# Reordering the second half of a two-layer graph-attention round: layer 0's second products inside v's, v's last products woven with the features', norm and adjacency moved

## The chip, the core and the metric

The kernel runs on one NeuronCore of a Trainium2 chip. The metric is the device time of one execution in microseconds (us), the median over several runs. TensorE (PE) multiplies, VectorE (DVE), ScalarE (ACT) and GpSimd (POOL) do the rest of the arithmetic, and SyncE (SP) issues the transfers. Each engine has its own queue of instructions and meets the others through semaphores.

## The reference

There are 64 graphs of 256 nodes with 512 features. Each passes through two layers, and each layer is `x = layernorm(x + gnn(x))`:

```python
# layer 0: graph attention, 8 heads of 64
feats = einsum('bnf,hfu->bhnu', X, W)
dense = leaky_relu(e_self[..., :, None] + e_neigh[..., None, :], 0.2)
att   = softmax(dense + NEG_BIG * (1.0 - A), axis=-1)
out   = relu(einsum('bhij,bhju->bhiu', att, feats) + b)
# layer 1: attention with adjacency and distance terms
q, k, v = split(x @ W_qkv)
attn = softmax(q k^T * scale) * 0.33 + 0.33 * adj + 0.33 * exp(-dist)
out  = (attn @ v) @ W_out + b_out
x = layernorm(x + out)
```

Both the adjacency and the distance matrix of layer 1 are the input `adj`. Everything is float32.

## The kernel before

The kernel is a software pipeline over the 64 graphs, written out by hand. A round of the main loop (`for b in range(NB)`, L1035) calls `attention0_beside_projections1(b)` (L877) and then `attention1_beside_projections0(b)` (L950). In one round several graphs are under way: layer 0's attention of graph b (`attend0`), layer 1's projections of graph b-1 (`proj1`), layer 0's projections of graph b+1 (`proj0`), the softmax of layer 1 for graph b-1 (`softmax1`) and its weighted sum for graph b-2 (`attend1`).

The order of the source is the order of the machine. `do(stage, b, step, ...)` (L857) emits one step and then calls `in_order()` (L86), which ties each new instruction to the one before it on the same engine. So every `do` line is a place in up to five queues, and moving a line moves its instructions in all of them. A step whose graph number lies outside 0 to 63 does nothing, which is how the pipeline fills and empties.

The three projections (q and k, v, and layer 0's features) are each made of seven block products instead of eight, `p1` to `p7`, by `seven` (L281). Their results share three PSUM banks. The bank called "chain" takes p1, p6, p7, p4 one after the other on top of each other, and after each of the four ScalarE copies the running sum out:

```python
BANK = dict(p1="chain", p6="chain", p7="chain", p4="chain", p2="alone", p5="pair", p3="pair")
COPIES = dict(p1=11, p6=12, p7=22, p4=21)
ADDED = {11: "alone", 22: "pair", 12: "pair"}
```

So p6 cannot start before ScalarE has copied p1, and so on along the chain. The bank called "pair" takes p5; VectorE's `add 22` reads it, and p3 may only then be added to it; `add 12` reads the sum. `add 11` reads "alone", which is p2. An `add` also needs the copy into the block of the same number. Matmuls of all projections are at L292, the copies at L301, the adds at L304. In the profile the tiles are `pq_p` for q and k, `pv_p` for v and `pf_p` for the features.

The PSUM banks of these products form a ring of four (`ps_tile`); each round takes 16, the last one only to bring the ring round. Two larger buffers (`sc`) alternate between layer 0's products and layer 1's scores.

The other steps that matter here:

- `attend0`: `weights(h)` (L520) writes a head's unnormalised attention `pT` on VectorE. `product(g, t)` (L539) multiplies for half g of the heads and half t of the nodes on TensorE. `norm0(g, t)` (L552, L554) divides on VectorE. `end` (L563) applies the relu and the residual on VectorE and then starts the mean on GpSimd (L338). `squares` (L343) sums squares on ScalarE and then calls GpSimd for the reciprocal root and shift (L350, L353, L354). `norm` (L358) applies the layer norm on ScalarE.
- `proj1`'s `blocks` stores the normed rows to DRAM (`hs`) and loads them back in blocks (`hb`); `hT` transposes them on VectorE (L121) for the next round's q and k products.
- `proj0`: `xT` transposes the next graph's input on VectorE (L121) and forms four differences (L268 to L271). `aT` transposes its adjacency on VectorE. `far` makes two exponentials of it on ScalarE and casts the mask (L384, L385, L387). `shared` (L393 to L408) uses the result on VectorE.
- `attend1`: `weights(g)` multiplies the exponentials p of a pair of heads by the reciprocal sums `rb` and adds `ct`, on VectorE (L750, L757). `values(g)` (L767) multiplies them with v on TensorE, and ScalarE copies every second result (`oT`, L775). `project` (L828) is the output projection.
- `softmax1`: `scores(g)` (L668) on TensorE, followed by its exponentials on ScalarE (L677). `both(g)` (L689) adds halves on VectorE. There are two buffers for the scores, so scores 2 and 3 wait until the exponentials of scores 0 and 1 have read them.

`load`, `load_adj` and `load_rows` fetch the next graphs' inputs, one buffer each, on SyncE's queue, which issues in order: an issue that waits holds back those behind it.

Of the kernel before, what the change touches and what calls it, by code (L numbers as in the profile page):

```python
# [17 lines left out]
def kernel(  # L18
# [31 lines left out]
    NB, N, F = x.shape  # L50
# [35 lines left out]
    def in_order():  # L86

        new = []
        for ins in reversed(nc.cur_bb.bb.instructions):
            if ins.name in traced:  # L90
                break
            traced.add(ins.name)
            new.append(ins)
        for ins in reversed(new):
            if ins.engine in last:
                tc.add_manual_dep(
                    ins,
                    last[ins.engine],
                    mybir.DependencyInfo(
                        mybir.DependencyClass.NoSync, mybir.DependencyReason.DATA  # L100
                    ),
                    reason="order of the source",
                )
            last[ins.engine] = ins.name
# [6 lines left out]
    def load_blocks(dst, src):  # L111

        for q in range(Q):
            nc.sync.dma_start(
                dst[q * B : (q + 1) * B],
                src.rearrange("(k r) (c q s) -> q r c k s", r=B, q=Q, s=B)[q],
            )
# [7 lines left out]
    def load(b):  # L125

        XB[b] = io.tile([P, C, N // B, B], FT, tag="xb", name=f"xb_{b}", bufs=1)
        load_blocks(XB[b], x[b])

    def load_adj(b):  # L130
        ADJB[b] = io.tile([P, T, N // B, B], FT, tag="adj", name=f"adj_{b}", bufs=1)
        load_blocks(ADJB[b], adj[b])
        MROW[b] = io.tile([P, N], U8, tag="mask", name=f"mask_{b}", bufs=4)
        nc.sync.dma_start(MROW[b], nodemask[b].partition_broadcast(P))

    def load_rows(b):
        X[b] = io.tile([P, T, F], FT, tag="x", name=f"x_{b}", bufs=1)
        nc.sync.dma_start(X[b], x[b].rearrange("(t p) f -> p t f", p=P))
# [605 lines left out]
    def attend1(b):  # L744
# [108 lines left out]
        proj0=proj0, attend0=attend0, proj1=proj1, softmax1=softmax1, attend1=attend1  # L853
# [3 lines left out]
    def do(stage, b, step, *args):  # L857

        if 0 <= b < NB:
            if (stage, b) not in S:  # L860
                S[stage, b] = stages[stage](b)
            S[stage, b][step](*args)
            in_order()
# [13 lines left out]
    def attention0_beside_projections1(b):  # L877


        do("attend1", b - 3, "squares")  # L880
        do("proj1", b - 1, "qk", "p1")
        do("proj1", b - 1, "qk", "p2")
        if b > 0:
            do("proj0", b, "columns")
        do("proj1", b - 1, "qk", "p6")
        for h in range(HG):
            if b > 0:
                do("proj0", b, "scaled", h)
            do("attend0", b, "weights", h)
        do("attend1", b - 3, "store")  # L890
        do("proj1", b - 1, "qk_add", 11)
        do("proj1", b - 1, "qk", "p5")
        do("proj1", b - 1, "qk", "p7")
        do("attend1", b - 2, "residual")
        do("proj1", b - 1, "qk_add", 22)
        do("attend0", b, "product", 0, 0)
        if b > 0:
            for h in range(HG, H):
                do("proj0", b, "scaled", h)
        do("proj1", b - 1, "qk", "p4")  # L900
        do("attend0", b, "product", 0, 1)
        do("attend1", b - 2, "weights", 0)
        for h in range(HG, H):
            do("attend0", b, "weights", h)
        do("attend0", b, "norm0", 0, 0)
        do("attend0", b, "norm0", 0, 1)
        do("proj1", b - 1, "qk", "p3")
        do("proj1", b - 1, "qk_add", 12)
        do("attend1", b - 2, "weights", 1)
        do("proj0", b + 1, "xT")  # L910
        if b + 2 < NB:
            load(b + 2)
        do("proj1", b - 1, "values", "p1")
        do("proj1", b - 1, "values", "p2")
        do("proj1", b - 1, "v_add", 11)
        do("proj1", b - 1, "values", "p6")
        do("proj1", b - 1, "values", "p5")
        do("proj1", b - 1, "values", "p7")
        do("proj1", b - 1, "v_add", 22)
        do("proj0", b + 1, "aT")  # L920
        if b + 2 < NB:
            load_adj(b + 2)
        do("attend0", b, "product", 1, 0)
        do("proj1", b - 1, "values", "p4")
        do("proj0", b + 1, "far")
        do("attend0", b, "product", 1, 1)
        do("attend0", b, "norm0", 1, 0)
        do("attend0", b, "norm0", 1, 1)
        do("proj0", b + 1, "product", "p1")
        do("proj1", b - 1, "values", "p3")  # L930
        do("proj1", b - 1, "v_add", 12)
        do("attend0", b, "end")
        do("proj0", b + 1, "product", "p6")
        do("proj0", b + 1, "product", "p5")
        do("proj0", b + 1, "product", "p7")
        do("proj0", b + 1, "product", "p2")
        do("proj0", b + 1, "add", 11)
        do("attend0", b, "squares")
        do("proj0", b + 1, "add", 22)
        do("attend1", b - 2, "weights", 2)  # L940
        do("proj0", b + 1, "product", "p4")
        do("attend0", b, "norm")
        do("proj1", b, "blocks")
        if b + 1 < NB:
            load_rows(b + 1)
        do("proj0", b + 1, "product", "p3")
        do("proj0", b + 1, "add", 12)
        do("attend1", b - 2, "weights", 3)

    def attention1_beside_projections0(b):  # L950
# [84 lines left out]
    for b in range(NB):  # L1035
        attention0_beside_projections1(b)
        if b == 0:
            combine_weights1()
            in_order()
        attention1_beside_projections0(b)  # L1040
# [49 lines left out]
```

The softmax here doesn't subtract the row's maximum and nothing guards it: scores larger than these inputs give would overflow.

## Time and profile before

The three runs took 3255.54, 3258.58 and 3258.8 us; the median is 3258.58. The profiled execution spans 3256.7 us at a granted TensorE clock of 0.988.

| | share of the span or time |
|---|---|
| TensorE on the chain that ended last | 71% |
| ScalarE on that chain | 10% |
| GpSimd on that chain | 7% |
| VectorE on that chain | 6% |
| ScalarE busy | 1459.7 us (45%) |
| GpSimd busy | 317.8 us (10%) |
| one round, from 1602.27 to 1651.44 us | 49.17 us |
| TensorE busy in that round | 48.84 us |
| VectorE busy in that round | 41.17 us |
| ScalarE busy in that round | 22.77 us |

The shares of the chain come from the profile's list of what ended last, followed back from release to release. The rows on one round come from a table of busy time by stretch. A round is best read in the timeline, where an engine's instructions stand in order of time, merged as long as they are of one kind: start, length, engine, line, operation, output and inputs, shapes, count, and in brackets the idle time ahead of it and what ended that. In the round shown, TensorE does the q and k products from 1607.24 us on, v's from 1623.42, layer 0's second half-products at 1627.74 and 1630.39, the features' from 1632.12, and the values and scores of layer 1 from 1639.67 to 1647.9. TensorE's ends are modelled, and a matmul that waits for the one before or for its weights may still count as busy, so it is safer to compare starts.

### The profile page before, as it was taken

Reading aid. Unit: us, or ns where it says so; the run is one execution under the profiler, and the core shown is the slowest. Engines: PE = TensorE matmul, PEld = TensorE weight load, DVE = VectorE, ACT = ScalarE, POOL = GpSimd, SP = SyncE. Lnnn points to the kernel's source line nnn. Section 1 sums busy time; section 2 is a strip of 40 time slices with the busy share of each in tenths; the row PEclk is TensorE's granted clock in tenths of the full one; section 3 lists DMA queues with packets and bytes.
Section 4 is the critical chain, followed back from the end, with each engine's and each line's share of the span. In section 5 each row is a group of like instructions: output and inputs, shape, how many; then the busy total and the mean of one; then the engine's idle time right before and its main releaser. Section 6 shows DMA issues by size and latency. Waiting matters only on the chain.

```text
span 3256.7 us, 55552 instructions
## 1 busy us (share of the span) xinstructions
PE 3160.1 (97%) x21262; PEld 2497.4 (77%) x21262; DVE 2653.1 (81%) x5152; ACT 1459.7 (45%) x3585; POOL 317.8 (10%) x518
## 2 busy tenths in 40 slices
PE   4999999999999999999999999999999999999997
PEld 4877877877877877778778778778778778788774
DVE  6688888888888878888888888888888888888874
ACT  1344444454454444444444444444444444444442
POOL 0001101011011011011011010110110110110110
PEclk7999999999999999999999999999999999999998
DMA  7244343443343443443443443434434434434421
GB/s 155 69 115 99 99 115 92 105 115 90 105 115 86 109 113 86 108 106 94 113 105 92 115 96 102 115 92 106 115 87 109 110 89 110 113 86 108 108 76 53
DMA packets 764393, 331.86 MB, mean 102 GB/s; under 512 B 696672, under 2 KB 697440, under 8 KB 747744
## 3 DMA queue, kind: packets, MB, share of 16 engines
q1 hardware_dynamic: 764128, 328.30, 39.8%
q8 instruction: 169, 2.77, 0.3%
q14 instruction: 96, 0.79, 0.1%
HBM read 259.80 MB, written 68.16 MB: 101 GB/s over the span
## 4 chain that ended last, share of the span: by engine, by line
PE 71%; ACT 10%; POOL 7%; DVE 6%; DMA 4%; issue 2%; SPq 1%; ACTq 0%; DVEq 0%; POOLq 0%
PE pq_p L292 22%; PE av L539 12%; PE po L828 12%; PE pv_p L292 11%; PE pf_p L292 7%; PE pz L668 4%; ACT junk L343 3%; POOL rstd_l L353 3%; ACT x L358 3%; ACT p L677 2%; POOL rstd_l L350 2%; POOL shift_l L354 2%; PE pd L697 2%; DMA gb<-gs 1%; DVE pT L520 1%
## 5 line engine op out<-in xcount | busy, mean ns | idle before, releaser
L539 PEld LDWEIGHTS av<-v,pT 128*128 128x128 f32 x4096 | 493.9, 194 | 18.9 <-ACT v L485 12.5
L539 PE MATMUL av<-v,pT 128*128 128x65 f32 x4096 | 491.8, 274 | 12.2 <-ACT v L485 12.2
L292 PE MATMUL pq_p<-hC,wqk_sb 128*128 128x128 f32 x4096 | 482.9, 276 | 1.7 <-ACT qk L301 1.6
L292 PEld LDWEIGHTS pq_p<-hC,wqk_sb 128*128 128x128 f32 x4096 | 467.8, 192 | 3.4 <-ACT qk L301 3.2
L828 PE MATMUL po<-wo_sb,oT 128*128 128x512 f32 x1008 | 460.1, 600 | 0.0
L520 DVE SCALAR_TENSOR_TENSOR pT<-gb,ccol,at 128x256 f32<-128x256 f32 x1024 | 416.9, 479 | 25.0 <-ACT ccol L448 17.9
L292 PE MATMUL pq_p<-hT,wqk_sb 128*128 128x128 f32 x3072 | 379.1, 281 | 9.2 <-DVE hT L121 9.2
L292 PEld LDWEIGHTS pq_p<-hT,wqk_sb 128*128 128x128 f32 x3072 | 358.3, 194 | 35.7 <-DVE hC L270 22.2
L301 ACT COPY v<-pv_p 128x256 f32<-128x256 f32 x256 | 95.3, 372 | 560.8 <-PE pv_p L292 560.8
L828 PEld LDWEIGHTS po<-wo_sb,oT 128*128 128x128 f32 x1008 | 181.9, 190 | 204.6 <-issue 203.2
L757 DVE TENSOR_TENSOR p<-p,ct 128x1024 f32<-128x1024 f32 x256 | 313.6, 1225 | 8.7
L750 DVE TENSOR_TENSOR p<-p,rb 128x1024 f32<-128x1024 f32 x256 | 311.1, 1215 | 7.0 <-DMA rb<-rs 7.0
L677 ACT ACTIVATE p<-pz,hide 128x512 f32<-128x512 f32 x512 | 312.0, 707 | 2.0 <-PE pz L668 1.9
L343 ACT ACTIVATE junk<-x,nmean_l 128x512 bf16<-128x512 f32 x256 | 184.9, 722 | 271.8 <-POOL nmean_l L338 267.7
L668 PE MATMUL pz<-qk 64*128 64x256 f32 x2048 | 274.3, 397 | 21.5 <-ACT p L677 20.2
L358 ACT ACTIVATE x<-x,shift_l,rstd_l 128x512 f32<-128x512 f32 x256 | 193.9, 805 | 223.7 <-POOL shift_l L354 223.7
L338 POOL TENSOR_SCALAR nmean_l<-sums_l 128x2 f32<-128x2 f32 x128 | 28.7, 224 | 2612.0 <-DVE x L563 1639.1
L668 PEld LDWEIGHTS pz<-qk 64*128 64x128 f32 x2048 | 183.0, 187 | 114.6 <-ACT p L677 75.0
L292 PE MATMUL pf_p<-wf_sb,xC 128*128 128x264 f32 x1008 | 254.1, 396 | 7.8 <-ACT v L301 4.5
L485 ACT ACTIVATE v<-v 128x64 f32<-128x64 f32 x1024 | 258.6, 340 | 0.0
L767 PE MATMUL av<-p,v 128*64 128x256 f32 x2016 | 245.8, 386 | 2.7 <-DVE p L757 2.7
L292 PE MATMUL pv_p<-wv_sb,hC 128*128 128x256 f32 x1024 | 242.1, 379 | 0.0
(107 smaller groups left out, 3970.4 us busy)
## 6 DMA issues: line engine op xcount, KB each, us to landing
gb<-gs SPq DMA_DIRECT2D x64, 1028.0 KB
rb<-rs SPq DMA_DIRECT2D x64, 1024.0 KB, 4.6
x<-in_x_dram SPq DMA_DIRECT2D x64, 512.0 KB, 4.2
hs<-x SPq DMA_DIRECT2D x64, 512.0 KB
hb<-hs SPq DMA_DIRECT2D x256, 128.0 KB, 3.1
out_dram<-x SPq DMA_DIRECT2D x64, 512.0 KB, 3.0
xb<-in_x_dram SPq DMA_DIRECT2D x252, 128.0 KB, 3.7
adj<-in_adj_dram SPq DMA_DIRECT2D x256, 64.0 KB, 3.0
```

The costliest lines, as they stand in the source:

```text
L292: matmul(d, lhsT, rhs, start=(p in FIRST and i == 0), stop=(i == len(todo) - 1), skip_group_check=True,)
L343: nc.scalar.activation(junk, self.src[:, t, :], AF.Square, bias=self.nmean[:, t : t + 1], accum_out=self.rstd[:, t : t + 1],)
L358: nc.scalar.activation(self.src[:, t, :], self.src[:, t, :], AF.Identity, bias=self.shift[:, t : t + 1], scale=self.rstd[:, t : t + 1],)
L485: nc.scalar.activation(V0[b][:, t, h, :U], V0[b][:, t, h, :U], AF.Copy, scale=V0[b][:, t, h, U : U + 1],)
L520: nc.vector.scalar_tensor_tensor(pT[h][:, j, :], GB[b][:, h, :N], CCOL[b][:, j, h : h + 1], AT[b][:, j, :], op0=ALU.max, op1=ALU.mult,)
L539: matmul(av[:, k, :], pT[h][:, j, t * P : (t + 1) * P], V0[b][:, j, h, :UA], start=(j == 0), stop=(j == T - 1),)
L668: matmul(pz[:, r, j, :], QK[b][rows, g, 1, j * P : (j + 1) * P], QK[b][rows, g, 0, :], start=True, stop=True,)
L677: nc.scalar.activation(p[:, :, j, :], pz[:, :, j, :], AF.Exp, bias=hide[:, j, b : b + 1], scale=U**-0.5,)
L750: nc.vector.tensor_mul(p, p, REC[b][:, k : k + 2, g // 2, :] .unsqueeze(2) .to_broadcast([P, 2, T, N]),)
L757: nc.vector.tensor_add(p, p, CT[b].unsqueeze(1).to_broadcast([P, 2, T, N]))
L767: matmul(av[0][r * U : (r + 1) * U, g % 2, :], V1[b][:, j, 2 * g + r, :], PROBS[b][g][:, r, j, :], start=(j == 0), stop=(j == T - 1),)
L828: matmul(po, oT[:, c, t * P : (t + 1) * P], wo_sb[:, c, :], start=(c == 0), stop=(c == C - 1),)
```

## The change

Only the order of the steps in the second half of `attention0_beside_projections1` changes; no step is added, dropped or altered.

- Layer 0's two second half-products move from behind v's p7 and p4 to behind v's p2 and p5. Their `norm0` and `end` follow at once, ahead of v's `add 22`.
- v's last products are woven with the features' first ones: p7, features' p1, p4, features' p6, p3.
- Layer 0's `squares` come before the features' p7, and its `norm`, the store of its rows and the load of the next rows come before the features' p2.
- The features' `add 22` comes before `add 11`.
- The adjacency's transpose, the load of the next adjacency and `far` move from v's p7 and p4 to behind the features' `add 11`.
- The second layer's `weights 1` move from ahead of `xT` to behind v's `add 12`; `weights 2` from ahead of the features' p4 to behind their p3.

It is meant to start layer 0's norm earlier, so that what waits for it on ScalarE and in memory is free sooner, and to give each chain copy another product to hide behind.

```diff
-        do("attend1", b - 2, "weights", 1)
         do("proj0", b + 1, "xT")
         if b + 2 < NB:
             load(b + 2)
         do("proj1", b - 1, "values", "p1")
         do("proj1", b - 1, "values", "p2")
         do("proj1", b - 1, "v_add", 11)
+        do("attend0", b, "product", 1, 0)
         do("proj1", b - 1, "values", "p6")
         do("proj1", b - 1, "values", "p5")
-        do("proj1", b - 1, "values", "p7")
-        do("proj1", b - 1, "v_add", 22)
-        do("proj0", b + 1, "aT")
-        if b + 2 < NB:
-            load_adj(b + 2)
-        do("attend0", b, "product", 1, 0)
-        do("proj1", b - 1, "values", "p4")
-        do("proj0", b + 1, "far")
         do("attend0", b, "product", 1, 1)
         do("attend0", b, "norm0", 1, 0)
         do("attend0", b, "norm0", 1, 1)
+        do("attend0", b, "end")
+        do("proj1", b - 1, "values", "p7")
+        do("proj1", b - 1, "v_add", 22)
         do("proj0", b + 1, "product", "p1")
+        do("proj1", b - 1, "values", "p4")
+        do("proj0", b + 1, "product", "p6")
         do("proj1", b - 1, "values", "p3")
         do("proj1", b - 1, "v_add", 12)
-        do("attend0", b, "end")
-        do("proj0", b + 1, "product", "p6")
+        do("attend0", b, "squares")
+        do("attend1", b - 2, "weights", 1)
         do("proj0", b + 1, "product", "p5")
         do("proj0", b + 1, "product", "p7")
-        do("proj0", b + 1, "product", "p2")
-        do("proj0", b + 1, "add", 11)
-        do("attend0", b, "squares")
-        do("proj0", b + 1, "add", 22)
-        do("attend1", b - 2, "weights", 2)
-        do("proj0", b + 1, "product", "p4")
         do("attend0", b, "norm")
         do("proj1", b, "blocks")
         if b + 1 < NB:
             load_rows(b + 1)
+        do("proj0", b + 1, "add", 22)
+        do("proj0", b + 1, "product", "p2")
+        do("proj0", b + 1, "add", 11)
+        do("proj0", b + 1, "aT")
+        if b + 2 < NB:
+            load_adj(b + 2)
+        do("proj0", b + 1, "product", "p4")
+        do("proj0", b + 1, "far")
         do("proj0", b + 1, "product", "p3")
         do("proj0", b + 1, "add", 12)
+        do("attend1", b - 2, "weights", 2)
         do("attend1", b - 2, "weights", 3)
```

## The prediction

> **What bounds the kernel now.** I read the page first. TensorE is busy nearly all the time and VectorE four fifths of it:
>
> ```profile
> PE 3160.1 (97%) x21262; PEld 2497.4 (77%) x21262; DVE 2653.1 (81%) x5152; ACT 1459.7 (45%) x3585; POOL 317.8 (10%) x518
> ```
>
> Busy is not unstalled, so I looked for the round in the PE timeline: the `pr` transposes start at 1602.27 and 1651.44, a round of 49.17 us. From the `pr` of 171.24 to that of 3131.70 lie 60 rounds, 49.34 us each. Then the waits view, and PE's timeline from 1636 to 1648:
>
> ```profile
> PE pz L668 <- ACT p L677: 20.2, 63, 2.9
> PEld pf_p L292 <- DVE v L304: 29.4, 63, 0.8
> DVE hT L121 <- DMA hb<-hs: 8.1, 8, 2.6
> ```
>
> ```profile
> 1636.60 1.94 PE L292 MATMUL pf_p<-wf_sb,xT 128*128 128x264 f32 x8
> 1638.58 1.16 PE L292 MATMUL pf_p<-wf_sb,xC 128*128 128x264 f32 x4
> 1639.67 1.95 PE L767 MATMUL av<-p,v 128*64 128x256 f32 x16
> 1641.55 2.00 PE L668 MATMUL pz<-qk 64*128 64x256 f32 x16
> 1643.48 1.95 PE L767 MATMUL av<-p,v 128*64 128x256 f32 x16
> 1645.69 2.29 PE L668 MATMUL pz<-qk 64*128 64x256 f32 x16 [0.26 <-ACT p L677]
> 1647.91 0.70 PE L828 MATMUL po<-wo_sb,oT 128*128 128x512 f32 x1
> ```
>
> Compare starts of like blocks. A feature product (4 matmuls) costs 0.89 us: the twelve from 1633.93 to 1636.60 took 2.67. But p2, p4, p3 took 3.07 (1636.60 to 1639.67); about 0.09 of it is the change to 64-column weights, so 0.31 is lost. The first two value blocks took 1.88, the second two 2.21: 0.33 lost. The first scores took 1.93, the second 2.22: 0.29 lost. So a round loses 0.93 us at two places: before the features' p3 (its weight load waits for VectorE's `add 22`), and at scores 2 and 3, which wait for the exponentials of scores 0 and 1. The causes stand in the VectorE, ScalarE and GpSimd timelines:
>
> ```profile
> 1637.76 0.77 DVE L304 TENSOR_TENSOR v<-pf_p,v 128x264 f32<-128x264 f32 x2 [1.99 <-PE pf_p L292]
> 1638.45 1.22 DVE L750 TENSOR_TENSOR p<-p,rb 128x1024 f32<-128x1024 f32 x1
> 1639.70 1.23 DVE L757 TENSOR_TENSOR p<-p,ct 128x1024 f32<-128x1024 f32 x1
> 1640.84 0.42 DVE L304 TENSOR_TENSOR v<-pf_p,v 128x264 f32<-128x264 f32 x1
> 1641.18 1.21 DVE L750 TENSOR_TENSOR p<-p,rb 128x1024 f32<-128x1024 f32 x1
> 1642.43 1.22 DVE L757 TENSOR_TENSOR p<-p,ct 128x1024 f32<-128x1024 f32 x1
> ```
>
> ```profile
> 1642.48 1.52 ACT L358 ACTIVATE x<-x,shift_l,rstd_l 128x512 f32<-128x512 f32 x2 [3.49 <-POOL shift_l L354]
> ```
>
> VectorE idles 1.99 us for `add 11` (it waits for p2), with `add 22` behind it; ScalarE's in-order queue is blocked 3.49 us by the layer norm waiting on GpSimd, and the exponentials stand behind it.
>
> **What the Trainium skill says.** "TensorE: Matmul & The Clock Gate", section "Architectural detail: the array is 16× 32×32, not 1× 128×128": TensorE's queue pulls weight loads ahead of running matmuls, while ScalarE and VectorE are strict first-in, first-out. The trace agrees: a late `add 22` costs a matmul slot through the load, and one late norm holds back all of ScalarE. "Perfetto Trace Analysis", section "Identifying the Most-Contended Engine": matmul busy time is a poor measure; so here, since the 0.93 us mostly count as busy. "GPSIMD Engine Reference", section "2. Architecture": GpSimd's SBUF port is shared with VectorE. The power at L353 takes 1.69 us beside VectorE's L750/L757, 0.71 at 1610.31; but L750 and L757 keep 1.21 to 1.23 us. So GpSimd pays, not VectorE.
>
> **The change, part by part.** No instruction is added or removed, so each queue's work is the same; every wait moves. I walk one round from v's p1 at 1623.42, with the trace's durations: v product 0.864 us, feature product 0.89, an attention half-product with the slower matmul after it 1.785; a PSUM reader starts 0.20 us after the next matmul block starts.
>
> TensorE after: v p1, p2 to 1625.15; first half-product to 1626.88 (its 0.054 falls in p6); p6, p5 to 1628.66; second half-product to 1630.39; p7 1631.31; f p1 1632.20; v p4 1633.07; f p6 1633.96; v p3 1634.82; f p5, p7, p2, p4 to 1638.38; f p3 to 1639.27, plus 0.09 is 1639.36, if nothing waits.
>
> Does anything there wait? The pT of heads 4 to 7 are done at 1623.69, before 1625.15. Each ScalarE copy that a chain needs (p1 before p6, p6 before p7, p7 before p4) has one product in between, 0.86 to 0.89, for 0.20 + 0.37: the same spacing as now, without loss (0.02 to 0.1 to spare for the load). v's p3 needs v's `add 22` at about 1632.8: met.
>
> VectorE after: attend1's weights 1 (2.39 us) leave the stretch before xT, so xT starts at 1625.31; xT 1.27, differences 1.48, `v_add 11` 0.33 to 1628.39; norm0 (1,0) 0.56; norm0 (1,1) waits for the second half-product, 1630.59, to 1631.15; `end` 1.24 to 1632.39; `v_add 22` to 1632.73; idle to 1635.02 for v p3; `v_add 12` to 1635.36; weights 1 to 1637.75; f `add 22`, ended at 1638.18. The load of f p3 wants it at 1638.16 and can take it 0.1 later: the 0.31 loss is gone, narrowly. f `add 11` to 1638.44, aT 0.70 to 1639.14, `add 12` after f p3 (1639.47) to 1639.81, weights 2 to 1642.20, weights 3 ended at 1644.67.
>
> That is the new wait. Before, weights 3 ended at 1643.65 and values 3 wanted it at about 1644.4. After, the unstalled value blocks run 1639.36 to 1641.24, scores 0, 1 to 1643.17, values 2 to 1644.09; then values 3 waits from 1644.09 to about 1644.73, with 0.05 more for the unprefetched load: 0.69 us. Behind it stand scores 2, 3, the projection and the next round.
>
> ScalarE after: f p6's copy ends 1634.51, squares to 1636.2, f p7's copy at 1636.80 on time; GpSimd's three operations take 1.25 us alone and 3.66 beside L750 (both in the trace), so the norm ends between 1638.9 and 1641.4 (1644.0 now); f p4's copy, far (1.47 us, moved behind the norm) to 1643.2 at worst; copy of oT, exponentials of scores 0 and 1 done by 1644.95 and 1646.1. The stalled PE reaches scores 2 and 3 at 1645.74 and 1646.71: no wait. So the 0.33 and 0.29 go too.
>
> Sum per full round: 0.93 removed, 0.69 added: 0.24 saved; with `add 12` 0.08 later (the reader after p2 now starts later by that), 0.16. I take 0.20, times 61 rounds (b = 2 to 62): 12 us.
>
> Irregular losses: 49.34 - 49.18 (the undisturbed round) over 60 rounds is 9.8 us. In most of these rounds `rb<-rs` or `hb<-hs` lands late. At 1816.44 a late rb held VectorE 1.40 us, so aT, so far, and f p1's copy behind far:
>
> ```profile
> 1832.11 2.94 PE L292 MATMUL pf_p<-wf_sb,xC 128*128 128x264 f32 x12 [0.98 <-ACT v L301]
> ```
>
> After, far is behind every copy but p3's, VectorE has 2.3 us of idle before v p3 to absorb it, and hb is asked for 2.6 us earlier. I book 8 us of the 9.8.
>
> Ends of the program: rounds 0 and 1 wait on hT (5.40 and 3.85 us in the PE timeline), which comes 2.0 and 2.6 us sooner with the earlier norm. In the last round, without features, weights 1 to 3 come later (1.5 us), but scores 2 waited 2.94 us for the norm, which comes 2.4 us earlier; net some 3 us. Together 8.
>
> The load of adj moves behind the rows' load on SP: SP is free from 1650.2 to 1653.8 now, and its five issues take 3.3 us, so `gs` is not held. Nothing.
>
> 3258.6 - 12 - 8 - 8 = 3230.6; I say 3230.
>
> **The rivals.** (1) VectorE is late at f p3 by some 0.3 us more than walked (the margin there is 0.1): then p3 stalls as now, weights 3 slip by the same, and the 0.20 per round becomes -0.10: 3258.6 + 6 - 16 = 3249. (2) The other side: a delay of 0.7 us in the VectorE chain, from GpSimd's operations now lying on weights 1 or from semaphore waits, makes each round 0.5 us longer: +30 - 16, 3273, slower. Against it: L750 and L757 keep their time beside GpSimd. (3) Values 3 never waits, because VectorE's idle after v p3 is shorter than I say: all 0.93 come back, 57 + 16 = 73 us: 3186. Against it: v p3 is an ordered wait, and 9.3 us of VectorE work stand between it and values 3.
>
> **How the numbers follow.** My walk 0.72; rival 1 0.15; rival 2 0.07; rival 3 0.06. An error of 0.15 us per round, the size of the margins, is 9 us; with the one-off terms (16, give or take 6) the range is 3214 to 3250. Faster by over 0.2% (below 3252) is the walk, rival 3 and half to two thirds of rival 1: 0.87; same 0.06; slower 0.07.
>
> **What would show it.** After: no `[... <-ACT p L677]` at scores 2; a new PE wait at av L767 on DVE p L757 of some 0.6 us, 60 times; PEld L292 waiting for DVE v L304 near zero; f p1's copy never behind far; the norm at L358 waiting less, hs some 2.6 us earlier; undisturbed rounds of 48.94 to 49.02. A wait at f p3 would mean rival 1; a round above 49.3, rival 2.

## The result, and the profile after

The changed kernel takes 3227.07 us in the median (3225.8 to 3228.24), against 3258.69 for the kernel before in the same comparison. The ratio is 0.9904, with a 95% interval of 0.9887 to 0.9921: 31.6 us, or 1%, faster. The prediction was 3230 with a range of 3214 to 3250.

The list of what ended last shows what became of the layer norm. ScalarE and GpSimd held 10% and 7% of that chain before; now both round to 0%:

```profile
PE 86%; DVE 11%; DMA 1%; SPq 1%; issue 1%; ACT 0%; POOL 0%; ACTq 0%; DVEq 0%; POOLq 0%
```

Here is TensorE's timeline of the same stretch of a round. v's p1 starts at 1605.50 here, against 1623.42 in the round of before, so 17.92 has to be added to compare:

```profile
1618.68 1.94 PE L292 MATMUL pf_p<-wf_sb,xT 128*128 128x264 f32 x8
1620.46 1.05 PE L292 MATMUL pf_p<-wf_sb,xC 128*128 128x264 f32 x4
1621.44 1.95 PE L767 MATMUL av<-p,v 128*64 128x256 f32 x16
1623.32 2.00 PE L668 MATMUL pz<-qk 64*128 64x256 f32 x16
1625.24 1.08 PE L767 MATMUL av<-p,v 128*64 128x256 f32 x8
1626.82 1.08 PE L767 MATMUL av<-p,v 128*64 128x256 f32 x8 [0.49 <-DVE p L757]
1627.83 2.00 PE L668 MATMUL pz<-qk 64*128 64x256 f32 x16
1629.76 0.70 PE L828 MATMUL po<-wo_sb,oT 128*128 128x512 f32 x1
```

The features' p2, p4 and p3 now take 2.76 us from start to start (1618.68 to 1621.44), not 3.07. Scores 2 and 3 take 1.93 and carry no wait for exponentials. But the second pair of value blocks, 1.88 us of work, takes 2.59 (1625.24 to 1627.83): values 3 waits. Its reason stands in VectorE's timeline:

```profile
1619.83 0.76 DVE L304 TENSOR_TENSOR v<-pf_p,v 128x264 f32<-128x264 f32 x2
...
1621.55 0.43 DVE L304 TENSOR_TENSOR v<-pf_p,v 128x264 f32<-128x264 f32 x1 [0.34 <-PE pf_p L292]
1621.90 1.22 DVE L750 TENSOR_TENSOR p<-p,rb 128x1024 f32<-128x1024 f32 x1
...
1625.54 1.23 DVE L757 TENSOR_TENSOR p<-p,ct 128x1024 f32<-128x1024 f32 x1
```

Weights 3 end at 1626.77 and values 3 starts at 1626.82. Over the whole program, in the waits view of the changed kernel:

```profile
PEld av L767 <- DVE p L757: 61.4, 63, 2.4
PE av L767 <- DVE p L757: 32.8, 63, 1.9
```

So the new wait comes once a round. The undisturbed round (the median) is 48.95 us where it was 49.18. Measured by the starts of `pr` in the two profiled executions, the 31.3 us between them split as follows: 6.5 us up to the fourth `pr` (the pipeline fills), 13.7 us from 60 rounds shorter by 0.228 each, 9.2 us from irregular losses (what single rounds take beyond the undisturbed one) that fell from 9.8 to 0.6, and 2.0 us at the end.

### The profile page after: what moved, and what is told of

The parts are those of the page before. It is cut to its first block, busy times and chain, and to the rows that moved or that the text cites. A ratio compares the mean times of both kernels' runs of the same rounds, so it can differ in the third digit from the quotient of the medians.

```text
span 3225.4 us, 56184 instructions
## 1 busy us (share of the span) xinstructions
PE 3129.4 (97%) x21262; PEld 2496.2 (77%) x21262; DVE 2642.8 (82%) x5152; ACT 1480.9 (46%) x3585; POOL 248.5 (8%) x518
## 4 chain that ended last, share of the span: by engine, by line
PE 86%; DVE 11%; DMA 1%; SPq 1%; issue 1%; ACT 0%; POOL 0%; ACTq 0%; DVEq 0%; POOLq 0%
PE pq_p L292 25%; PE po L828 14%; PE av L539 14%; PE pv_p L292 12%; PE pf_p L292 12%; DVE p L757 5%; DVE p L750 5%; PE pz L668 4%; PE av L767 2%; PE pd L697 2%; PE pr L82 1%; DVE v L304 1%; SPq L236 0%; DMA gb<-gs 0%; PE po L810 0%
## 5 line engine op out<-in xcount | busy, mean ns | idle before, releaser
L520 DVE SCALAR_TENSOR_TENSOR pT<-gb,ccol,at 128x256 f32<-128x256 f32 x1024 | 416.8, 479 | 24.0 <-ACT ccol L448 17.9
L757 DVE TENSOR_TENSOR p<-p,ct 128x1024 f32<-128x1024 f32 x256 | 313.5, 1225 | 8.7
L750 DVE TENSOR_TENSOR p<-p,rb 128x1024 f32<-128x1024 f32 x256 | 311.5, 1217 | 7.7 <-DMA rb<-rs 7.6
L767 PE MATMUL av<-p,v 128*64 128x256 f32 x2016 | 260.0, 389 | 32.8 <-DVE p L757 32.8
L292 PE MATMUL pv_p<-wv_sb,hC 128*128 128x256 f32 x1024 | 259.3, 386 | 0.3 <-DVE v L304 0.3
L668 PE MATMUL pz<-qk 64*128 64x256 f32 x2048 | 256.9, 390 | 0.6 <-ACT p L677 0.6
L767 PEld LDWEIGHTS av<-p,v 128*64 128x64 f32 x2016 | 128.1, 136 | 149.4 <-DVE p L757 61.4
```

The source lines that it names most:

```text
L292: matmul(d, lhsT, rhs, start=(p in FIRST and i == 0), stop=(i == len(todo) - 1), skip_group_check=True,)
L520: nc.vector.scalar_tensor_tensor(pT[h][:, j, :], GB[b][:, h, :N], CCOL[b][:, j, h : h + 1], AT[b][:, j, :], op0=ALU.max, op1=ALU.mult,)
L668: matmul(pz[:, r, j, :], QK[b][rows, g, 1, j * P : (j + 1) * P], QK[b][rows, g, 0, :], start=True, stop=True,)
L750: nc.vector.tensor_mul(p, p, REC[b][:, k : k + 2, g // 2, :] .unsqueeze(2) .to_broadcast([P, 2, T, N]),)
L757: nc.vector.tensor_add(p, p, CT[b].unsqueeze(1).to_broadcast([P, 2, T, N]))
L767: matmul(av[0][r * U : (r + 1) * U, g % 2, :], V1[b][:, j, 2 * g + r, :], PROBS[b][g][:, r, j, :], start=(j == 0), stop=(j == T - 1),)
```

## The experiments

Theory at this point, as in the prediction: three losses of the kernel before are gone (0.31 us at the features' p3, 0.33 and 0.29 at scores 2 and 3), and one of about 0.7 has come in their place, VectorE's chain into values 3. The rivals: the losses of before are not as I divided them; the moves of the weights are what pays; far's place is what counts. "Round" below is the median distance of two `pr` transposes in the profiled execution. The kernel before took 3256.5 to 3258.9 us beside each of these runs, so times of different runs can be set side by side.

### Weights 1 back in front, weights 2 into VectorE's idle time

The changed order with these edits:

```diff
+        do("attend1", b - 2, "weights", 1)
         do("proj0", b + 1, "xT")
...
-        do("attend0", b, "end")
         do("proj1", b - 1, "values", "p7")
         do("proj1", b - 1, "v_add", 22)
+        do("attend0", b, "end")
...
-        do("attend1", b - 2, "weights", 1)
+        do("attend1", b - 2, "weights", 2)
...
         do("proj0", b + 1, "add", 12)
-        do("attend1", b - 2, "weights", 2)
         do("attend1", b - 2, "weights", 3)
```

> The changed order, but with layer 1's weights 1 back ahead of xT, weights 2 where weights 1 had been put (behind v's add 12), and v's add 22 ahead of the layer 0 end. Theory (in the changed kernel the only steady loss on TensorE, 0.71 us a round, is values 3 waiting for weights 3 on VectorE): weights 3 end some 2.4 us sooner, values 3 does not wait, a round takes 48.24 us instead of 48.95, and the time is about 3184 us. Rival A (the exponentials of scores 0 and 1 are the next wait, right behind): scores 2 and 3 wait again and most of the 0.71 us stays, about 3215 to 3227. Rival B (the norm, 0.5 us later on VectorE, sets the end): no better than 3227.

Measured: 3186.68 us, ratio to before 0.9779 (0.9766 to 0.9793), a round of 48.24. Its TensorE timeline has no wait left in this stretch, and the second pair of value blocks takes 1.88 us again:

```profile
1603.49 2.00 PE L668 MATMUL pz<-qk 64*128 64x256 f32 x16
1605.41 1.95 PE L767 MATMUL av<-p,v 128*64 128x256 f32 x16
1607.29 2.00 PE L668 MATMUL pz<-qk 64*128 64x256 f32 x16
```

The whole 0.71 us a round came back, as expected if the wait for weights 3 was the one steady loss of this stretch. This version beats both kernels: 2.2% below before, 40 us below the changed one. Its irregular losses are 1.1 us, although weights 1 stand in front again.

### The change without its moves of the weights

```diff
+        do("attend1", b - 2, "weights", 1)
         do("proj0", b + 1, "xT")
...
-        do("attend1", b - 2, "weights", 1)
...
             load_adj(b + 2)
+        do("attend1", b - 2, "weights", 2)
...
         do("proj0", b + 1, "add", 12)
-        do("attend1", b - 2, "weights", 2)
         do("attend1", b - 2, "weights", 3)
```

> The changed order without its moves of layer 1's weights: weights 1 ahead of xT and weights 2 behind the features' add 11 and aT, as in the kernel before. Theory: weights 2 and 3 still run mostly after v p3, but only 4.9 us of them; weights 3 end about 1626.1 on the changed kernel's clock, where values 3 wants them at 1625.95 to 1626.16; a wait of about 0.2 us is left, and v's p3 may wait 0.1 us for add 22; a round of 48.5 us, about 3200 us. Rival (the moves of the weights are what pays for the gain): slower than 3227.

Measured: 3191.66 us, ratio 0.9793 (0.978 to 0.9807), round 48.24. The direction is as expected; the waits of 0.2 and 0.1 us that I had left in do not show. The 60 rounds hold 7.2 us of irregular losses, though, where the changed kernel has 0.6. In each of its ten disturbed rounds TensorE stands at v's p3, which waits for `add 22`. So the moves of the weights cost 35 us net within the change, and what they gave for it is that late transfers hardly matter any more. The first experiment has nearly the same without them: there `add 22` stands ahead of layer 0's `end`, and 1.1 us are lost.

### Only the moves of the weights, in the kernel before

```diff
-        do("attend1", b - 2, "weights", 1)
         do("proj0", b + 1, "xT")
...
         do("attend0", b, "end")
+        do("attend1", b - 2, "weights", 1)
...
-        do("attend1", b - 2, "weights", 2)
...
         do("proj0", b + 1, "add", 12)
+        do("attend1", b - 2, "weights", 2)
         do("attend1", b - 2, "weights", 3)
```

> The kernel before with only the moves of layer 1's weights: weights 1 behind the layer 0 end, weights 2 behind the features' add 12. Theory: p3 waits 0.3 us longer for add 22, and values 3 waits for weights 3 some 0.6 us, while scores 2 and 3 wait no more; a round gains about 0.37 us, 23 us in all, less some 6 us of irregular waits that the slack on VectorE ahead of aT takes away: 3270 to 3282. Rival (VectorE's weights are hidden, only the norm counts): 3258 or faster.

Measured: 3274.19 us, ratio 1.0047 (1.0034 to 1.0059), round 49.58. The round is 0.40 longer (0.37 expected), and the irregular losses fall from 9.8 to 0.1 us although far stays where it was. Which transfer is late stands in VectorE's rows, at L443. First a long round of the kernel before (50.15 us), then an undisturbed one (49.58) of this run:

```profile
1069.78 0.18 DVE L443 TENSOR_TENSOR nd<-v,gb 128x16 f32<-128x16 f32 x1 [2.87 <-DMA gb<-gs]
```

```profile
531.19 0.19 DVE L443 TENSOR_TENSOR nd<-v,gb 128x16 f32<-128x16 f32 x1 [2.67 <-DMA gb<-gs]
```

Usually this wait is 1.2 us. Of the 16 rounds of before that are over 0.08 us too long, eight have `gb<-gs` late by 0.5 to 2.1 us (5.8 us lost in them), five `hb<-hs` (2.1 us) and one `rb<-rs` (1.2 us); the other two lose 0.6 us. Here `gb` is late by 0.6 to 1.8 us in eight rounds, which lose 0.2 us together. So weights 1 behind the end of layer 0 is enough to make the kernel nearly indifferent to a late transfer.

### Only the order of two adds, in the kernel before

```diff
         do("proj0", b + 1, "product", "p7")
+        do("proj0", b + 1, "add", 22)
         do("proj0", b + 1, "product", "p2")
         do("proj0", b + 1, "add", 11)
         do("attend0", b, "squares")
-        do("proj0", b + 1, "add", 22)
```

> The kernel before with one edit: the features' add 22 ahead of add 11 (and ahead of p2). Theory: the 0.31 us that the features' p3 loses goes, but TensorE then waits that much longer at scores 2 and 3 for the exponentials, which stand behind the layer norm on ScalarE; the time stays at 3258 us within 3. Rival (the losses add up, each is worth its own 0.31 us a round): 3240 us.

Measured: 3233.28 us, ratio 0.9918 (0.9904 to 0.9931), round 48.77. Both expectations fell. I had said nothing would come of it; one moved line brings 25.6 us, more even than the 19 of the rival. The norm must have ended earlier, and it did: it starts 18.65 us after v's p1 (1627.26 less 1608.61), against 19.06 before (1642.48 less 1623.42). These 0.41 us are the gain of the round: on TensorE the 0.31 us ahead of p3 are gone, and the second values and scores, which still wait for the exponentials, lose 0.52 us instead of 0.62. GpSimd's timelines say why the norm moved. First the kernel before, then this one:

```profile
1638.82 0.90 POOL L350 TENSOR_SCALAR rstd_l<-rstd_l 128x2 f32<-128x2 f32 x1 [2.74 <-ACT junk L343]
1639.80 1.69 POOL L353 TENSOR_TENSOR rstd_l<-rstd_l,mhalf 128x2 f32<-128x2 f32 x1
1641.57 0.88 POOL L354 TENSOR_TENSOR shift_l<-nmean_l,rstd_l 128x2 f32<-128x2 f32 x1
```

```profile
1624.01 0.48 POOL L350 TENSOR_SCALAR rstd_l<-rstd_l 128x2 f32<-128x2 f32 x1 [2.74 <-ACT junk L343]
1624.58 1.69 POOL L353 TENSOR_TENSOR rstd_l<-rstd_l,mhalf 128x2 f32<-128x2 f32 x1
1626.35 0.88 POOL L354 TENSOR_TENSOR shift_l<-nmean_l,rstd_l 128x2 f32<-128x2 f32 x1
```

and VectorE's rows of this one beside them:

```profile
1623.23 1.21 DVE L750 TENSOR_TENSOR p<-p,rb 128x1024 f32<-128x1024 f32 x1
1624.48 1.22 DVE L757 TENSOR_TENSOR p<-p,ct 128x1024 f32<-128x1024 f32 x1
...
1625.96 1.22 DVE L750 TENSOR_TENSOR p<-p,rb 128x1024 f32<-128x1024 f32 x1
```

Compare ends. L350 ends at 1624.49, VectorE's L750 at 1624.44. L354 ends at 1627.23, the next L750 at 1627.17. In the kernel before L350 ends at 1639.72 and L750 at 1639.67. I looked at all of them: of the instructions at L350 and L354 that overlap one of VectorE's L750 or L757, 125 of 125 in the kernel before end 50 ns (to the nearest 10) after it. L353 ends some 0.57 us after the one it overlaps at its start. So GpSimd's three small operations do not take a fixed time beside VectorE, as I had priced them; each is held until the L750 or L757 of the moment has ended, and the norm goes when the third of them has. As long as the three fall on the same instructions, whatever shifts weights 2 shifts the norm, the exponentials and scores 2 and 3. `add 22` behind the wait of `add 11` had delayed weights 2 by 0.41 us.

### A useless instruction ahead of weights 2, in the kernel before

The new theory makes an odd forecast. If VectorE is kept on something that does not hold GpSimd while L350 runs, one weights instruction fewer lies before the norm.

```diff
         do("proj0", b + 1, "add", 22)
+        probe(b)
         do("attend1", b - 2, "weights", 2)
```

Here `probe` issues `nc.vector.tensor_reduce(t, bo_bc[:, :384], AX.X, ALU.max)` in rounds 2 to 62; nothing reads `t`.

> The kernel before plus one useless VectorE instruction a round (a maximum over 128x384 into one column, about 0.57 us) just ahead of layer 1's weights 2. New theory after swap_only (the norm ends late because GpSimd's L350, L353 and L354 each have to wait until VectorE's running L750 or L757 ends; in every profiled run so far L350 and L354 ended 50 ns after it): L350 now finishes in the gap ahead of L750, one L750/L757 fewer lies before the norm, which ends some 0.9 us sooner although VectorE has more to do; scores 2 and 3 wait no more, a round takes 48.56 to 48.66 us and the time is 3222 to 3232 us: an added instruction makes the kernel faster. Rival A (GpSimd follows weights 2, whatever lies ahead): every round 0.57 us longer, 3293. Rival B (VectorE's delay is hidden, and the norm takes its fixed time): 3259.

Measured: 3216.91 us, ratio 0.9872 (0.9859 to 0.9886), round 48.55. The added instruction makes the kernel 40 us faster. VectorE and then GpSimd in this kernel:

```profile
1617.91 0.54 DVE L881 TENSOR_REDUCE probe<-bo_bc 128x1 f32<-128x384 f32 x1
1618.37 1.22 DVE L750 TENSOR_TENSOR p<-p,rb 128x1024 f32<-128x1024 f32 x1
1619.62 1.23 DVE L757 TENSOR_TENSOR p<-p,ct 128x1024 f32<-128x1024 f32 x1
```

```profile
1618.28 0.19 POOL L350 TENSOR_SCALAR rstd_l<-rstd_l 128x2 f32<-128x2 f32 x1 [2.74 <-ACT junk L343]
1618.55 1.60 POOL L353 TENSOR_TENSOR rstd_l<-rstd_l,mhalf 128x2 f32<-128x2 f32 x1
1620.23 0.67 POOL L354 TENSOR_TENSOR shift_l<-nmean_l,rstd_l 128x2 f32<-128x2 f32 x1
```

L350 takes its 0.19 us in the shadow of the reduction, L353 is held by the first L750, and L354 ends 50 ns after L757 (1620.90 and 1620.85), not after the next L750. The norm starts 18.05 us after v's p1, 1.0 us earlier. The features' p2, p4 and p3 still take 3.07 us here (1616.06 to 1619.13) and the second values and scores 1.88 and 1.92: the 0.63 us of the round are the scores' loss alone. That the hold exists is shown. What in L750 and L757 makes it is not: they read two SBUF inputs and the reduction one, and the Trainium skill's "GPSIMD Engine Reference", section "1. Specifications", names VectorE instructions with two SBUF inputs, or in a mode with two ports, as those that contend. The traces agree with that, though no run was made to vary it alone. In the changed kernel L354 runs inside the transpose of the adjacency, which has one input, in all of 61 overlaps, and keeps its 0.20 us; the 0.22 us of L338 fall into v's `add 22`, which has one of its two inputs in PSUM, 63 times, and are not stretched either:

```profile
1620.51 0.70 DVE L121 STREAM_TRANSPOSE adjT<-adj 128x512 f32<-128x512 f32 x1
```

```profile
1620.56 0.20 POOL L354 TENSOR_TENSOR shift_l<-nmean_l,rstd_l 128x2 f32<-128x2 f32 x1
```

In the kernel with the two adds swapped, L354 fell three times inside yet another instruction with two SBUF inputs (L253, L393 and L520, of 1024, 512 and 256 columns) and each time ended 54 to 55 ns after it. At L393:

```profile
114.38 0.68 DVE L393 TENSOR_TENSOR ct<-adjT,far 128x512 f32<-128x512 f32 x1
```

```profile
114.45 0.67 POOL L354 TENSOR_TENSOR shift_l<-nmean_l,rstd_l 128x2 f32<-128x2 f32 x1
```

So neither the length of L750 and L757 nor anything peculiar to them is needed.

### The same two adds, put back in the changed kernel

```diff
-        do("proj0", b + 1, "add", 22)
         do("proj0", b + 1, "product", "p2")
         do("proj0", b + 1, "add", 11)
+        do("proj0", b + 1, "add", 22)
```

> The changed kernel with the features' add 22 back behind add 11. Theory: here the norm no longer sets the end but VectorE's chain into values 3 does; p3 waits 0.31 us for add 22, add 12 and weights 2 and 3 slip by the same: a round of 49.26 us, 3246 us. Rival (the wait at values 3 swallows the wait at p3): 3227.

Measured: 3247.13 us, ratio to before 0.9972 (0.996 to 0.9984), round 49.27. That is 0.32 us a round over the changed kernel: here the swap is worth its own stall at p3, because the norm no longer lies on the path. The same edit is worth 0.41 us where the norm sets the end and 0.32 through the weight load where it does not.

### A useless addition on VectorE, late and early in the changed kernel

Here `probe` issues `nc.vector.tensor_add(t, bo_bc, bo_bc)`, 128x512, in rounds 2 to 62. First late, behind the features' p3:

```diff
         do("proj0", b + 1, "add", 12)
+        probe(b)
         do("attend1", b - 2, "weights", 2)
```

> The changed kernel plus one useless 128x512 VectorE addition a round (0.61 us by the rows of that size) between the features' add 12 and weights 2. Theory (VectorE's chain from p3 through weights 3 sets values 3): each of 61 rounds longer by 0.61 us, 3264 us. Rival (VectorE has slack there): 3227.

Measured: 3263.73 us, ratio to before 1.002 (1.0012 to 1.0029), round 49.55: 0.60 longer. Then early, where VectorE waits for v's p3:

```diff
         do("proj1", b - 1, "v_add", 22)
+        probe(b)
         do("proj0", b + 1, "product", "p1")
```

> The changed kernel plus the same useless addition between v's add 22 and add 12, where VectorE sits idle 1.68 us for v's p3. Theory: nothing, 3227 us within 3. Rival (VectorE's total work sets the time): 3264.

Measured: 3228.87 us, ratio to before 0.9914 (0.9901 to 0.9928), round 48.95, unchanged. The same instruction, 0.68 us long in its record with its overlap, costs 0.60 us a round behind p3 and nothing ahead of v's p3.

### The weave undone, in the changed kernel

```diff
         do("proj1", b - 1, "v_add", 22)
-        do("proj0", b + 1, "product", "p1")
         do("proj1", b - 1, "values", "p4")
-        do("proj0", b + 1, "product", "p6")
+        do("proj0", b + 1, "product", "p1")
         do("proj1", b - 1, "values", "p3")
         do("proj1", b - 1, "v_add", 12)
+        do("proj0", b + 1, "product", "p6")
```

> The changed kernel without the weave of v's last products: p7 and p4 stand together again with no other product between, then the features' p1, v's p3, the features' p6. Theory (each link of a chain costs a ScalarE copy: 0.20 us to its start and 0.37 us, hidden only by one product in between): p4 waits about 0.62 us and loses 0.1 more on its unprefetched weights, all behind it slips by the same, VectorE's chain into values 3 too: 0.73 us a round, 3271 us. Rival (the slip is taken up by the wait at values 3): 3227.

Measured: 3274.31 us, ratio to before 1.0055 (1.004 to 1.007), round 49.68: 0.73 over the changed kernel, as worked out. That is what one uncovered link of a chain, p7 to p4, costs here.

### far back beside v's products, in the changed kernel

```diff
         do("proj1", b - 1, "v_add", 22)
+        do("proj0", b + 1, "aT")
+        if b + 2 < NB:
+            load_adj(b + 2)
         do("proj0", b + 1, "product", "p1")
         do("proj1", b - 1, "values", "p4")
+        do("proj0", b + 1, "far")
...
-        do("proj0", b + 1, "aT")
-        if b + 2 < NB:
-            load_adj(b + 2)
         do("proj0", b + 1, "product", "p4")
-        do("proj0", b + 1, "far")
```

> The changed kernel with aT and far back where they were beside v's products (aT behind v's add 22, far behind v's p4). Theory: aT is free there, but far's 1.47 us now stand on ScalarE between the copies of v's p4 and the features' p6; the features' p7 waits about 0.4 us, squares and the copies behind them slip, p4 waits some 0.3 us more, and with it p3, add 12 and values 3: a round of 49.4 to 49.6 us, 3252 to 3268 us. Rival (far's place does not matter): 3227.

Measured: 3249.32 us, ratio to before 0.9975 (0.9965 to 0.9984), round 49.25: 0.30 over the changed kernel, where I had 0.45 to 0.65. ScalarE copies the features' p6 1.3 us later, behind far, and p7 waits for that; the second wait, at p4, is nearly hidden. The irregular losses stay at 0.6 us, so with weights 1 in their later place they do not depend on far's.

## Why the prediction was right

**The walk of the round held to a few hundredths where it counts.** On the clock of the prediction (17.92 added), f `add 22` ended at 1638.17 (1638.18 predicted), weights 3 at 1644.69 (1644.67), and values 3 started at 1644.74 (1644.73). The norm ended at 1640.23, between the two bounds given. The round shrank by 0.228, between 0.16 and 0.24; I took 0.20. That makes 13.7 us over 60 rounds (12 over 61 predicted). One step of VectorE's walk was wrong. `norm0 (1,0)` was to run at 1628.39, ahead of the second half-product; it waited for it, as it does in the kernel before, and began at 1630.59. So v's `add 22` ended at 1633.34, not 1632.73, and the idle time ahead of v's p3 was 1.68 us, not 2.3. That idle time took up the error; that it was there to do so was foreseen, the error was not.

**The price of the new wait was right and is shown.** The late and early probes, and weights 1 and 2 taken out of the chain into values 3, all came within 3 us of what that chain predicts.

**The losses removed were right in sum and wrong as separate causes.** I treated the 0.31 at p3 and the 0.62 at scores as independent and GpSimd's 3.66 us as a fixed price "beside L750". In the kernel before they are tied: the late `add 22` also delays weights 2, and weights 2 and 3 hold GpSimd and with it the norm. The swap alone showed it, the added reduction confirmed it. The forecast did not depend on it, because the change takes the norm off the path altogether: its bound of 1641.4 for a slow GpSimd still left the exponentials on time.

**The irregular losses were sized well, and their causes were half misnamed.** I booked 8 us, 9.2 came. I said that `rb<-rs` or `hb<-hs` lands late in most of these rounds and showed one with `rb`; in the kernel before that is the only one, and `gb<-gs` is the late transfer in half of them. Where it holds VectorE up, though, the path is the one I gave, by the adjacency and far to the copy of the features' p1, and the size came near. Of the two remedies that I named, far's place does not matter once weights 1 stand later. With the weights moved alone the losses go, so the slack that weights 1 leave on VectorE is enough. It is not the only way: with weights 1 in front and `add 22` ahead of layer 0's `end`, 1.1 us are lost. For `hb` the run with the added reduction speaks: there the norm comes 1.0 us earlier, weights 1 keep their place, and none of the 60 rounds waits for `hb` by more than 0.3 us, against five in the kernel before.

**The ends**: 8 us booked, 8.5 measured (6.5 at the start, 2.0 at the end); the split was 5 and 3.

None of the rivals came about. The margin that rival 1 turned on was narrow but sufficient: the weights of p3 loaded without a wait, and putting `add 22` back produced the stall that it feared.

## What to carry to other kernels

When an engine's order is fixed by hand, walk the two or three chains around the moved lines with the durations of the trace, and look first at what the change leaves last: here it took 0.93 us off a round and put 0.71 back, because weights 2 and 3 were moved behind a product that ends late. With weights 1 left in front, weights 2 put into VectorE's idle time and `end` behind `add 22`, the new order gave 72 us where the change gave 32. A stall seen at one instruction may also be feeding another; undo it alone before adding it up.

## What the runs showed that I had not expected

- A GpSimd operation of 0.19 us on a 128x2 tile took 0.35 to 1.25 us beside VectorE's L750 or L757 in the kernel before, because it ended 50 ns after that instruction: the price is what is left of it. L353, 0.71 us alone, ended 0.57 us after it. Beside VectorE's transposes and its adds out of PSUM it lost nothing.
- So VectorE instructions off the critical path can set the end through GpSimd, and an added instruction of 0.54 us made the kernel 40 us (1.3%) faster.
- Moving one line, `add 22` ahead of p2, gave 26 us by itself, where the whole change gave 32.
- The rounds that a late transfer disturbs are mostly those with `gb<-gs` late, by up to 2.1 us, and moving `weights 1` and `weights 2` took the irregular losses from 9.8 us to 0.1.
